# Attention and graph mixing on one core: another place for a run's last blocks, and x centred row by row on ScalarE

## The chip, the cores and the metric

One core of a Trainium2 chip runs the whole computation. The metric is the device time of one execution in microseconds. Engines work side by side, each on its own queue of instructions: TensorE (PE, with its weight loads PEld) multiplies matrices, VectorE (DVE) and ScalarE (ACT) do elementwise work and row sums, GpSimd (POOL) does the powers and starts most transfers, SyncE (SP) starts transfers and here also passes marks between TensorE instructions. Engines wait for each other by semaphores.

## The reference

Two layers over x of 16 batches x 1024 nodes x 64 channels and a dense 1024 x 1024 matrix adj, all in float32:

```python
Q = einsum('bnc,oc->bno', x, Wq) + bq
K = einsum('bnc,oc->bno', x, Wk) + bk
V = einsum('bnc,oc->bno', x, Wv)
score = softmax(einsum('bnc,bmc->bnm', Q, K), axis=1)
out = einsum('bnm,bmc->bnc', einsum('bnm,mc->bnc', score, adj), V)
x = layernorm(x + out)
# layer 1, with support0 = support1 = adj
x1 = adj @ x;  x2 = 2 * adj @ x1 - x
out = concat([x, x1, x2, x1, x2]) @ weight + bias
x = layernorm(x + out)
```

layernorm takes the mean of a node's 64 channels away and divides by the standard deviation; it has no weights.

## The kernel before, in words

**Data.** Two batches are kept together as a pair p, 0 to 7, so a tile of x for one pair is 128 nodes x (8 node blocks x 2 batches x 64 channels). `rows(p)` sees it as 16 rows of 64 channels on each of the 128 partitions. Batch j of a pair lies on partitions 64j to 64j+63 of the transposed tiles.

**The attention loop** (L699 to L785) runs over steps (p, m): pair p, column block m of its scores, 63 steps. The product adj @ x stands in place of adj @ V; the value weights are applied behind it. Step (p, m) prepares the scores of the next step for both batches (`sc0` for j = 0, `sc1` for j = 1, each 128 x 1024 in PSUM), and uses the exponentials of its own. For each batch VectorE takes the maximum (L409) and ScalarE the exponential (L418), which also sums it. Of both sums VectorE makes the reciprocal `ri` (L425) and the scaled weights `us` (L427), with which TensorE accumulates the attention result (`weighted`, L439). The score tile of one batch is the same buffer in every step, so the scores of step m + 1 wait for the exponential of step m.

**TensorE in quarters.** All products of the loop are 64 x 64: an instruction reads partitions 0 to 63 or 64 to 127 (here called row half 0 and row half 1) and writes one column half. Scores of batch 0 and the weighted products with t = 0 use row half 0, those of batch 1 and t = 1 row half 1.

**Beside the attention** the same steps carry, each a piece at a time and written out in order by hand:

- a `Run` (L673): one block product of adj @ x or of the next hop, by a scheme with seven products in place of eight. `part(t, *ks)` issues the blocks ks of row half t. When the last blocks of t = 0 are out, `passed` (L662) puts an instruction on SyncE's queue that waits for them and raises a mark; the first blocks of t = 1, which add into the same bank, wait for that mark (`behind_mark`, L669). VectorE evicts the run in the next step (L293 to L299).
- a small product, `small_of` (L653): `values` at (p, 1), `project` at (p, 4), `mix` at (p, 0), (p, 2), (p, 3), (p, 5) from p = 2 on. It is made for batch 0 (`small0`) in the first half of the step and for batch 1 (`small1`) in the second half, both in the one bank that the run doesn't hold. The second waits until ScalarE and VectorE have taken the first out (`project`: L381 and L385), and the run of the next step takes the same bank.
- VectorE jobs in two dictionaries by step, `first_gap` and `second_gap` (L625): sums for the block scheme (L250), transposes (L346), and the layer norms: the mean of x before the attention result is added (`means`, L391), its removal (`centre`, L394), the variance (L480), the scaling (L496). In a step the jobs of `first_gap` stand on VectorE between the maxima of batch 0 and batch 1.

In six steps (`two_runs`) two runs are made and no small product.

**Order on ScalarE in a step:** evictions of a small product of batch 0, the exponential of batch 0, in (p, 7) a copy (L504), evictions of the small product of batch 1, the exponential of batch 1.

**Behind the loop** (from 408 us) the second layer's hops run as full-size products; that part is not touched. There L993 scales single rows of 64 channels on ScalarE.

Of the kernel before, what the change touches and what calls it, by code (L numbers as in the profile page):

```python
# [10 lines left out]
AF = mybir.ActivationFunctionType  # L11
# [15 lines left out]
def gnn_kernel(  # L27
# [13 lines left out]
    nc = tc.nc  # L41
    N, B, C = out.shape
    P = 128
    K8 = N // P
    NP = B // 2
    HP = NP // 2
    H = 512
    G = 16
# [27 lines left out]
    def f_other(name):  # L76

        return pf.tile([P, H], FP, tag=f"f{1 - f_last[0]}", name=name)

    def sc_tile(name):  # L80
        return psc.tile([P, N], FP, tag="sc", name=name)
# [153 lines left out]
    class Hop:  # L235
# [46 lines left out]
        def evict(self, po, n, group, copy=nc.vector.tensor_copy):  # L282
            for do in self.evictions(po, n, group, copy):
                do()
# [23 lines left out]
    XT, GT, ACC, PU, OT, SQ, RSTD, X0T, XM = ({} for _ in range(9))  # L308

    def by_block(t):  # L310

        return t.rearrange("c (k a n) -> c a k n", k=K8, a=A4)

    def by_place(t):
        return t.rearrange("c (a k n) -> c a k n", k=K8, a=A4)
# [8 lines left out]
    def rows(p):  # L324
        return xs[:, p].rearrange("p k (b c) -> p (k b) c", b=2)

    def xT(p):
        if p not in XT:
            XT[p] = att.tile([P, N], FP, tag="xT", name="xT")
        return XT[p]  # L330
# [11 lines left out]
    def transposed(p, dst, queue=nc.gpsimd):  # L342


        t = att.tile([P, N], FP, tag="t", name="blocks", bufs=1)
        nc.vector.transpose(  # L346
            t.rearrange("p (b k n) -> p k b n", b=A4, k=K8),
            xs[:, p].rearrange("p k (b n) -> p k b n", b=A4),
        )
        d = dram.tile([P, N], FP, tag="d", name="d")  # L350
        queue.dma_start(d, t)  # L351
        for b in range(A4):
            queue.dma_start(
                dst[32 * b : 32 * b + 32].rearrange("c (a w) -> c a w", a=A4),
                d.rearrange("(a c) (b w) -> b c a w", a=A4, b=A4)[b],
            )
# [36 lines left out]
    def centre(p):  # L393
# [2 lines left out]
            op0=ALU.mult, op1=ALU.add,  # L396
        )

    def scores(sc, p, m, j, h):

        for c in range(2):
            nc.tensor.matmul(  # L402
                sc[half[c], ts(h, H)], GT[p][half[j], c * H + m * C : c * H + (m + 1) * C],
                xT(p)[half[j], ts(h, H)], start=True, stop=True,
            )
# [15 lines left out]
    def scaled(p, m):  # L421

        es, sm = PU[p, m]
        ri = small.tile([P, 2], FP, tag="ri", name="ri")
        nc.vector.reciprocal(ri, sm)  # L425
        us = small.tile([P, 2, C], FP, tag="us", name="us")
        nc.vector.tensor_tensor(  # L427
            us, UY[:, m, ts(p, P)].rearrange("p (j c) -> p j c", j=2),
            ri[:, :, None].to_broadcast([P, 2, C]), ALU.mult,
        )  # L430
        PU[p, m] = (es, us)

    def weighted(p, m, t, h):

        if m == 0 and t == 0:
            ACC[p, h] = pacc.tile([P, H], FP, tag=f"acc{h}", name="acc")
        es, us = PU[p, m]
        made = [
            nc.tensor.matmul(  # L439
                ACC[p, h][half[j]], us[half[t], j], es[j][half[t], ts(h, H)],  # L440
                start=m == 0 and t == 0, stop=m == K8 - 1, skip_group_check=True,
            )
            for j in range(2)
        ]
        if h == 0 and (t or m):
            behind_mark(made, sum_mark.pop())
        if h == 1 and not (t and m == K8 - 1):
            sum_mark.append(passed(made))

    def attended(p, h):  # L450

        if h == 0:
            OT[p] = att.tile([P, N], FP, tag="oT", name="oT", bufs=1)
        nc.scalar.activation(half_block(OT[p], h), half_place(ACC.pop((p, h))), AF.Copy)
# [31 lines left out]
    def squared(p):  # L486
        SQ[p] = att.tile([P, G, C], FP, tag="t", name="sq", bufs=1)
        nc.scalar.activation(SQ[p], rows(p), AF.Square, scale=C**-0.5)
# [13 lines left out]
    def x0T_in_order(p):  # L502
        t = att.tile([P, N], FP, tag="o", name="x0T_k", bufs=1)
        nc.scalar.activation(by_block(t), by_place(X0T[p]), AF.Copy)  # L504
        X0T[p] = t
# [78 lines left out]
    bias = const.tile([P, C], FP, tag="bias", name="bias")  # L584
# [37 lines left out]
        runs += [(hop, n, g) for order, groups in orders for g in groups for n in order]  # L622
    two_runs = {(0, 1), (0, 2), (1, 0), (2, 7), (HP + 1, 6), (HP + 1, 7)}

    first_gap, second_gap = {}, {}  # L625

    def at(gap, step, do, *args):
        gap.setdefault(step, []).append(lambda: do(*args))
# [10 lines left out]
        at(first_gap, step, hop_z.sums, n)  # L639
    for p in range(NP):  # L640

        at(first_gap, {
            0: (0, 6), 1: (1, 0), 2: (2, 1), 3: (3, 1), 6: (HP + 1, 7), 7: (7, 1)
        }.get(p, (p, 0)), means, p)
        at(first_gap, {0: (1, 0)}.get(p, (p, 6)), centre, p)
        if p + 1 < NP:
            at(first_gap, (p + 1, 2), spread, p)
            at(first_gap, (p + 1, 3), normed, p)
            at(first_gap, (p + 1, 5 if p + 2 < NP else 4), x0T, p)
        if p + 2 < NP:  # L650
            at(first_gap, (p, 7), lambda p: transposed(p, xT(p)), p + 2)
# [47 lines left out]
    for p in range(NP):  # L699
        q = p - 1  # L700
        for m in range(K8):
            if (p, m) == (NP - 1, K8 - 1):
                break
            nxt = (p, m + 1) if m + 1 < K8 else (p + 1, 0)
            sc = sc_tile("sc0")
            scores(sc, *nxt, 0, 0)
            rest = []
            if tail:
                tail.part(1, 2, 3)
                rest = tail.evict()  # L710
            scores(sc, *nxt, 0, 1)
            if before:
                weighted(*before, 1, 0)
                if m == 0:
                    attended(q, 0)
            scaled(p, m)
            for evict in late:
                evict()
            late = []
            if m == 2 and p:  # L720
                squared(q)
            todo = [Run() for _ in range(2 if (p, m) in two_runs else 1)]
            if before:
                weighted(*before, 1, 1)
                PU.pop(before)
            todo[0].part(0, 0, 1)
            what = small_of.get((p, m))
            sc1 = sc_tile("sc1")
            if what:
                parts, by_scalar, by_vector = what[0](*what[1:], (0,), [f_other("small0")])  # L730
                parts[0]()
            scores(sc1, *nxt, 1, 0)
            if what:
                for do in parts[1:]:
                    do()
            else:
                todo[0].part(0, 2, 3)
            nm = maximum(sc)
            if m == 0 and before:
                attended(q, 1)  # L740
            if what:
                by_scalar()
            exps(*nxt, 0, sc, nm)
            if p and m == (7 if p < NP - 1 else 6):
                x0T_in_order(q)
            jobs = first_gap.get((p, m), []) + rest
            if what:
                jobs.insert(len(jobs) if what[0] is project else 0, by_vector)
            for do in jobs:
                do()  # L750
            scores(sc1, *nxt, 1, 1)
            if what:
                todo[0].part(0, 2, 3)
            elif len(todo) > 1:
                todo[1].part(0, 0, 1)
                todo[1].part(0, 2, 3)
                todo[0].part(1, 0, 1)
            nm = maximum(sc1)
            weighted(p, m, 0, 0)
            if what:  # L760
                parts, by_scalar, by_vector = what[0](*what[1:], (1,), [f_other("small1")])
                if what[0] is project:
                    todo[0].part(1, 0)
                parts[0]()
                by_scalar()
                exps(*nxt, 1, sc1, nm)
            elif len(todo) > 1:
                todo[0].part(1, 2, 3)
                exps(*nxt, 1, sc1, nm)
                for do in todo[0].evict():  # L770
                    do()
            else:
                exps(*nxt, 1, sc1, nm)
            weighted(p, m, 0, 1)
            if what:
                for do in parts[1:]:
                    do()
                by_vector()
            if what and what[0] is project:
                todo[0].part(1, 1)  # L780
            else:
                todo[-1].part(1, 0, 1)
            for do in second_gap.get((p, m), ()):
                do()
            tail, before = todo[-1], (p, m)  # L785
# [384 lines left out]
    for step_, (i, cols) in enumerate((  # L1170
# [3 lines left out]
        k, p, n = wide_step(4, 1, 0, i, cols)  # L1174
# [49 lines left out]
```

## Time and profile before

| what | value |
|---|---|
| time, median of 4 runs | 569.97 us (569.59 to 570.35) |
| profiled execution | 569.59 us, its span 567.8 us |
| TensorE clock granted, mean | 0.993 |
| TensorE busy | 98% |
| VectorE busy | 78% |
| ScalarE busy | 44% |
| GpSimd busy | 27% |
| L394, centring on VectorE | 8 x 1216 ns |
| L391, means on VectorE | 8 x 1206 ns |
| attention loop, first to last step | 35.6 to 408 us of the span |

Times in the timeline are microseconds from the start of the span: start, duration, engine, line, operation, result <- inputs, shapes, count; in brackets how long the engine stood idle before and for whom. A row of PE may hold two instructions, the two column halves, and rows of the two row halves overlap.

### The profile page before, as it was taken

What the parts mean: (1) busy time and instruction counts of PE and PEld (TensorE: products, weight loads), DVE (VectorE), ACT (ScalarE), POOL (GpSimd) and SP (SyncE); (2) the same over time, 40 slices, a digit from 0 to 9 for tenths busy, and PEclk for the clock granted to TensorE, in tenths of its full rate; (3) what the DMA queues carried; (4) which work ended last, traced back from release to release, by engine and by line L of the source; (5) the groups of instructions that cost most, each with busy time, mean ns of one, the idle gap of its engine ahead of it and who ended that gap; (6) DMA issues with size and microseconds to landing.
All of it is one profiled execution on the core that took longest, in us unless ns stands there. A gap on an engine that the chain in (4) does not pass through costs nothing.

```text
span 567.8 us, 14491 instructions
## 1 busy us (share of the span) xinstructions
PE 555.6 (98%) x6150; PEld 410.1 (72%) x6150; DVE 441.8 (78%) x722; ACT 249.7 (44%) x525; POOL 153.1 (27%) x145
## 2 busy tenths in 40 slices
PE   9999999999999999999999999999999999999992
PEld 7757677657677877767767786577678789888552
DVE  1789889788888988879788788898656565799784
ACT  1133454546656556555654655455532200141571
POOL 0001001211211202112121120102102994793784
PEclk9999999999999999999999999999999999999997
DMA  8902001022012003102201200200102400002943
GB/s 277 331 2 76 2 39 39 1 76 76 3 66 86 2 1 114 38 2 76 76 1 52 101 1 3 75 2 15 64 1 75 76 0 2 1 21 53 208 142 95
DMA packets 20994, 33.66 MB, mean 59 GB/s; under 512 B 3010, under 2 KB 12482, under 8 KB 20546
## 3 DMA queue, kind: packets, MB, share of 16 engines
q0 software_dynamic: 6880, 18.88, 11.5%
q1 hardware_dynamic: 14050, 13.86, 7.4%
q8 instruction: 48, 0.79, 0.6%
q14 instruction: 16, 0.13, 0.1%
HBM read 16.48 MB, written 12.06 MB: 50 GB/s over the span
## 4 chain that ended last, share of the span: by engine, by line
PE 89%; DVE 5%; ACT 2%; DMA 1%; issue 1%; SPq 0%; POOL 0%; POOLq 0%; ACTq 0%; DVEq 0%
PE p L268 20%; PE sc L402 18%; PE acc L439 17%; PE w L831 15%; PE small L517 3%; PE w L1139 3%; PE pu L258 3%; PE wide L831 3%; PE small L464 2%; PE small L367 2%; DVE nm L409 1%; PE pv L258 1%; PE p L258 1%; ACT e L418 1%; PE both L517 1%
## 5 line engine op out<-in xcount | busy, mean ns | idle before, releaser
L402 PE MATMUL sc<-xT,GT 64*64 64x512 f32 x1024 | 240.8, 591 | 0.4 <-ACT e L418 0.2
L439 PE MATMUL acc<-e,us 64*64 64x512 f32 x1008 | 239.6, 590 | 0.0
L418 ACT ACTIVATE e<-sc,nm 128x1024 f32<-128x1024 f32 x128 | 142.8, 1115 | 123.3 <-DVE nm L409 115.6
L409 DVE TENSOR_REDUCE nm<-sc 128x1 f32<-128x1024 f32 x128 | 155.6, 1216 | 2.6 <-PE sc L402 2.1
L439 PEld LDWEIGHTS acc<-e,us 64*64 64x64 f32 x1008 | 71.0, 133 | 23.9 <-issue 9.2
L483 POOL TENSOR_TENSOR rstd<-var,expo 128x16 f32<-128x16 f32 (+3 forms) x21 | 50.8, 2427 | 130.7 <-DVE var L481 130.6
L402 PEld LDWEIGHTS sc<-xT,GT 64*64 64x64 f32 x1024 | 69.7, 132 | 12.0 <-issue 5.2
L351 POOL DMA_DIRECT2D d<-blocks x14 | 8.4, 599 | 198.5 <-DVE blocks L346 198.5
L268 PE MATMUL p<-UY,aT 64*64 64x256 f32 x480 | 59.2, 377 | 0.0
L268 PE MATMUL p<-XB,S 64*64 64x256 f32 x480 | 57.8, 377 | 0.0
L268 PE MATMUL p<-UY,S 64*64 64x256 f32 x384 | 45.7, 378 | 0.0
L268 PE MATMUL p<-XB,aT 64*64 64x256 f32 x352 | 43.4, 377 | 0.0
L268 PEld LDWEIGHTS p<-UY,aT 64*64 64x64 f32 x480 | 33.6, 133 | 12.1 <-issue 1.8
L268 PEld LDWEIGHTS p<-XB,S 64*64 64x64 f32 x480 | 33.0, 133 | 12.2 <-issue 2.3
L517 PE MATMUL small<-w,x0T_k 64*64 64x192 f32 x384 | 39.7, 323 | 0.0
L517 PEld LDWEIGHTS small<-w,x0T_k 64*64 64x64 f32 x384 | 26.7, 133 | 12.5 <-issue 5.5
L268 PEld LDWEIGHTS p<-UY,S 64*64 64x64 f32 x384 | 27.2, 133 | 8.4 <-issue 1.2
L268 PE MATMUL p<-xs,aT 64*64 64x256 f32 x256 | 31.7, 378 | 0.0
L268 PEld LDWEIGHTS p<-XB,aT 64*64 64x64 f32 x352 | 25.5, 133 | 8.5 <-issue 1.9
L268 PE MATMUL p<-xs,S 64*64 64x256 f32 x256 | 31.1, 377 | 0.0
L844 ACT COPY own<-w 128x512 f32<-128x512 f32 x8 | 4.5, 588 | 54.6 <-PE w L831 54.6
L527 ACT ACTIVATE UY<-small 128x128 f32<-128x128 f32 x48 | 13.3, 278 | 31.0 <-PE small L517 31.0
(210 smaller groups left out, 944.7 us busy)
## 6 DMA issues: line engine op xcount, KB each, us to landing
d<-blocks POOLq DMA_DIRECT2D x14, 512.0 KB, 3.0
xs<-own POOLq DMA_DIRECT2D x8, 512.0 KB, 6.8
xT<-d POOLq DMA_DIRECT2D x28, 128.0 KB, 2.9
x0T<-d POOLq DMA_DIRECT2D x28, 128.0 KB, 2.9
out_dram<-xs SPq DMA_DIRECT2D x14, 256.0 KB, 2.2
xs<-in_x_dram SPq DMA_DIRECT2D x3, 1024.0 KB, 7.6
aT<-in_adjT_dram SPq DMA_DIRECT2D x8, 256.0 KB, 4.8
aT<-in_adjT_dram SPq DMA_DIRECT2D x4, 512.0 KB, 7.7
```

Source lines behind the costliest of these rows:

```text
L258: nc.tensor.matmul(po[t * w : (t + 1) * w], SIDE[n][:, k, j : j + w], self.side[n][:, :, k, :], start=start, stop=True, skip_group_check=True,
L268: nc.tensor.matmul(po[half[c]], SIDE[n][half[t], k, i * P + c * C : i * P + (c + 1) * C], self.side[n][half[t], :, k, :], start=t == 0 and ...
L367: nc.tensor.matmul(t[half[b]], g2[half[j], half[j]], xT(p)[half[j], ts(b, H)], start=True, stop=True,)
L402: nc.tensor.matmul(sc[half[c], ts(h, H)], GT[p][half[j], c * H + m * C : c * H + (m + 1) * C], xT(p)[half[j], ts(h, H)], start=True, stop= ...
L409: nc.vector.tensor_reduce(nm, sc, AX.X, ALU.max, negate=True)
L418: nc.scalar.activation(e, sc, AF.Exp, bias=nm, accum_out=sm[:, j : j + 1])
L439: nc.tensor.matmul(ACC[p, h][half[j]], us[half[t], j], es[j][half[t], ts(h, H)], start=m == 0 and t == 0, stop=m == K8 - 1, skip_group_che ...
L483: nc.gpsimd.tensor_tensor(rstd, var, expo[:, 0:n], ALU.pow)
L517: nc.tensor.matmul(t[half[c], 0:3, k], X0T[p][half[j], n : n + C], w3[half[j]], start=True, stop=True,)
L527: nc.scalar.activation(part(UY, j), t[:, 0], AF.Copy)
L831: nc.tensor.matmul(po[:, ts(g, b.shape[1] * P)], a[:, k, ts(g, P)], b[:, :, k, :], start=start and g == 0 and k == 0, stop=True, skip_grou ...
L1139: nc.tensor.matmul(po, SIDE[n][:, k, ts(i, P)], B_F[n][:, k, cols], start=k == 0, stop=k == K4 - 1)
```

## The change

Three things change.

1. In a step with a small product, the run's last blocks of the first half, `part(0, 2, 3)` on row half 0, are issued ahead of `scores(sc1, ..., 1, 1)` on row half 1 instead of behind them. Steps without a small product had this order already.
2. x of pairs 1 to 7 is centred by ScalarE in place of VectorE. ScalarE multiplies the 16 row sums by -1/64 and then handles each row of 64 channels in an instruction of its own, with the mean as a bias per partition: 8 rows in (p, 1) and 8 in (p, 6), for pair 7 in (7, 1) and (7, 4). In a step they are issued behind the exponential of batch 0 and ahead of the evictions and the exponential of batch 1. Pair 0 stays on VectorE.
3. The row sums (`means`) are taken in other steps: for pairs 2 to 6 at (p - 1, 6), for pair 7 at (5, 0); pairs 0 and 1 stay at (0, 6) and (1, 0).

```diff
+    def centre_rows(p, b):
+
+        if b == 0:
+            nc.scalar.mul(XM[p], XM[p], -1.0 / C)
+        for i in range(G // 2 * b, G // 2 * (b + 1)):
+            nc.scalar.activation(rows(p)[:, i], rows(p)[:, i], AF.Identity, bias=XM[p][:, i : i + 1])
...
-        at(first_gap, {
-            0: (0, 6), 1: (1, 0), 2: (2, 1), 3: (3, 1), 6: (HP + 1, 7), 7: (7, 1)
-        }.get(p, (p, 0)), means, p)
-        at(first_gap, {0: (1, 0)}.get(p, (p, 6)), centre, p)
+        at(first_gap, {0: (0, 6), 1: (1, 0), 7: (HP + 1, 0)}.get(p, (p - 1, 6)), means, p)
+        if p == 0:
+            at(first_gap, (1, 0), centre, p)
+        else:
+            for b, m in enumerate((1, 6 if p + 1 < NP else 4)):
+                at(scalar_gap, (p, m), centre_rows, p, b)
...
             if p and m == (7 if p < NP - 1 else 6):
                 x0T_in_order(q)
+            for do in scalar_gap.get((p, m), ()):
+                do()
             jobs = first_gap.get((p, m), []) + rest
             if what:
                 jobs.insert(len(jobs) if what[0] is project else 0, by_vector)
             for do in jobs:
                 do()
-            scores(sc1, *nxt, 1, 1)
             if what:
                 todo[0].part(0, 2, 3)
-            elif len(todo) > 1:
+            scores(sc1, *nxt, 1, 1)
+            if len(todo) > 1:
                 todo[1].part(0, 0, 1)
                 todo[1].part(0, 2, 3)
                 todo[0].part(1, 0, 1)
```

`HP` is 4, `NP` 8, `G` 16, `C` 64; `scalar_gap` is a third dictionary by step.

More of the change, by code (lines that the diff above doesn't have):

```diff
@@ L623, in gnn_kernel @@
     two_runs = {(0, 1), (0, 2), (1, 0), (2, 7), (HP + 1, 6), (HP + 1, 7)}
-    first_gap, second_gap = {}, {}
+    first_gap, second_gap, scalar_gap = {}, {}, {}
     def at(gap, step, do, *args):
```

## The prediction

> **What bounds the kernel now.** I read the page's busy shares first, then the groups, the waits, and last the timeline of single steps of the attention loop, which fills 35.6 to 408 us of the span.
>
> ```profile
> PE 555.6 (98%) x6150; PEld 410.1 (72%) x6150; DVE 441.8 (78%) x722; ACT 249.7 (44%) x525; POOL 153.1 (27%) x145
> L418 ACT ACTIVATE e<-sc,nm 128x1024 f32<-128x1024 f32 x128 | 142.8, 1115 | 123.3 <-DVE nm L409 115.6
> L993 ACT ACTIVATE xs<-xs,rstd 128x64 f32<-128x64 f32 x64 | 15.8, 342 | 6.3 <-POOL rstd L483 6.3
> L394 DVE SCALAR_TENSOR_TENSOR xs<-xm,xs 128x1024 f32<-128x1024 f32 x8 | 9.7, 1216 | 0.0
> PEld p L268 <- SPq L664: 6.5, 17, 0.8
> ```
>
> PE is busy 98%, so only places where it stands still or runs on one row half can give time. A busy PE may be on one half only: products on row half 0 and row half 1 run beside each other. I added, step by step, the starts' spacings (512 columns 0.43 us, 256 columns 0.215, 192 columns 0.16, two column halves at once) and compared with each step's length. Steps with mix products lose about 0.03 us; steps with values 0.2; with project 0.28, and the step behind project 0.31. Steps (6,6) to (7,1) lose 2.1 together: there VectorE runs without a pause.
>
> This is PE's timeline in project step (4,4), the second part of it:
>
> ```profile
> 249.43 0.41 PE L268 MATMUL p<-XB,S 64*64 64x256 f32 x2
> 249.58 0.59 PE L402 MATMUL sc<-xT,GT 64*64 64x512 f32 x2
> 250.01 0.59 PE L402 MATMUL sc<-xT,GT 64*64 64x512 f32 x2
> 250.08 0.41 PE L268 MATMUL p<-XB,S 64*64 64x256 f32 x2
> 250.44 0.59 PE L402 MATMUL sc<-xT,GT 64*64 64x512 f32 x2
> 251.23 0.43 PE L268 MATMUL p<-XB,S 64*64 64x256 f32 x2
> 251.71 0.59 PE L367 MATMUL small<-xT,g 64*64 64x512 f32 x2
> ```
>
> and, of its weight loads:
>
> ```profile
> 251.23 0.20 PEld L268 LDWEIGHTS p<-XB,S 64*64 64x64 f32 x4 [0.76 <-SPq L664]
> ```
>
> The blocks p of 249.43 to 250.08 are the run's last blocks of the first half (row half 0). In the code they stand behind all scores of row half 1 (starts 249.58 to 250.44), yet start before the last of them. The blocks at 251.23 (row half 1) wait for SyncE's mark (`passed`, L662) of the first ones. Those were over by 250.08 + 0.38 = 250.46, but the mark comes only after the scores are over, 250.44 + 0.59 = 251.03. So starts pass each other between row halves, while completion is reported in the order of the code. Row half 1 is free at 250.44 + 0.43 = 250.87 and stands until 251.23.
>
> And this is the loop that links the steps, in (4,6) and (4,7), the centring of x[4] on VectorE (L394) included:
>
> ```profile
> 262.09 1.22 DVE L394 SCALAR_TENSOR_TENSOR xs<-xm,xs 128x1024 f32<-128x1024 f32 x1
> 262.29 1.11 ACT L418 ACTIVATE e<-sc,nm 128x1024 f32<-128x1024 f32 x1 [1.87 <-DVE nm L409]
> 263.32 1.23 DVE L409 TENSOR_REDUCE nm<-sc 128x1 f32<-128x1024 f32 x1
> 264.64 1.11 ACT L418 ACTIVATE e<-sc,nm 128x1024 f32<-128x1024 f32 x1 [1.14 <-DVE nm L409]
> 265.88 0.17 DVE L425 RECIPROCAL ri<-es 128x2 f32<-128x2 f32 x1
> 266.29 1.22 DVE L409 TENSOR_REDUCE nm<-sc 128x1 f32<-128x1024 f32 x1
> 267.63 1.11 ACT L418 ACTIVATE e<-sc,nm 128x1024 f32<-128x1024 f32 x1 [1.78 <-DVE nm L409]
> 268.88 0.14 PEld L402 LDWEIGHTS sc<-xT,GT 64*64 64x64 f32 x2
> ```
>
> The second exponential (264.64, sums read until 265.84) releases the reciprocal at 265.88; behind it on VectorE stands the next maximum (266.29), which releases the next first exponential (267.63 to 268.74), which frees the score bank that PE writes at 268.88. PE could have begun at 268.78 (the product of 268.35 plus 0.43). This chain has no slack.
>
> **Part 1, the order on PE.** It touches the 38 steps with small products (7 values, 7 project, 24 mix). No product is added or removed, and on each row half the order stays. In mix steps the halves are already full. In a project step the mark now follows scores that end at 249.58 + 0.59 = 250.17 and blocks that end at 250.46, so it is there before 250.87: row half 1 gains 251.23 - 250.87 = 0.36. The small product behind it (251.71) moves to 251.35, unless its bank is late: the VectorE copy of the first half's result ends at 250.38 + 0.76 = 251.14, in time. ScalarE's copy (252.78) and VectorE's second copy (253.50), and so the bank for which row half 0 waits in the next step (254.31), follow by 0.36. Both halves gain 0.36. In p = 2, 3, 5 and 6 the first copies end at 156.56, 204.73, 297.61 and 347.50, each over 0.4 before the small product at 157.15, 205.25, 298.18 and 348.06: same gain. In p = 0 and 1 these copies end at 64.98 and 110.62, right before the small products at 65.03 and 110.73: nothing. Sum 5 x 0.36 = 1.8 us gained. From below: nothing, if another wait takes the mark's place; from above 7 x 0.36 = 2.5.
>
> A rule speaks here. The Trainium skill's page "TensorE: Matmul & The Clock Gate", section "The mechanism" of Part 3, says that matmuls start and end strictly in program order and only weight loads are pulled ahead. By it the old order would hold row half 0 from about 249.43 until 250.44, the new one would not, and 0.4 us in each of 38 steps, 15 us, would be an estimate of the gain. The starts above contradict the first half of it; the late mark agrees with the second.
>
> **Part 2, x centred by ScalarE.** VectorE loses seven L394, 7 x 1.216 = 8.5 us. ScalarE gets 112 rows of 128x64 and seven products of 128x16. The nearest row is L993, the same shape in place with one operand per partition: 16 take 3.95 us, so (3.95 - 0.34) / 15 = 0.24 apart. From below, L527 and L528 (128x128 with constants) start 0.16 apart; from above, 0.34, if nothing overlaps. I take 0.24, the same form and shape.
>
> The rows stand on ScalarE between the two exponentials of a step. The next instruction starts 1.10 behind the first exponential (267.63 to L504 at 268.73), eight rows take 8 x 0.24 = 1.92: the second starts at least 3.02 behind the first. Before, at (p,6): p = 1: 121.37 to 123.62, 2.25; p = 2: 2.45; p = 3: 215.83 to 218.18, 2.35; p = 4: 2.35; p = 5: 3.38; p = 6: 2.91; p = 7 at (7,4): 394.53 to 396.88, 2.35. Late by 0.77, 0.57, 0.67, 0.67, 0, 0.11, 0.67.
>
> The chain above passes this on to PE: p = 1 at (2,0) 0.77 (old start 127.86, PE free 127.84); p = 3 and 4 0.67 each; p = 6 0.11. For p = 2 the step (2,7) has two runs: the exponential of 173.06 to 174.17 frees the bank 1.7 before PE needs it at 175.94, so nothing. For p = 7 a wait for PE hides most: the first exponential of 399.84 starts at 400.51, ends at 401.62 and frees the bank 0.13 later (268.74 to 268.88 above), PE wants it at 401.65: 0.1. Sum 0.77 + 2 x 0.67 + 0.11 + 0.1 = 2.3 us lost.
>
> At (p,1) the second exponential comes 2.43 behind the first (231.97 to 234.40) and would come 3.13 behind (0.11 more for the small product); the 0.7 is covered, because the reciprocal of (4,2) waits for PE's blocks until 236.37 anyway and the late sums are there at 236.30. If that cover were gone, 7 x 0.7 = 4.9 would show.
>
> **Part 3, the means.** Same seven reductions of 1.21, now mostly at (p-1,6), where L394 stood, so (1,6) to (5,6) carry the same VectorE work. Relieved are (2,1), (3,1), (4,0), (5,7), (6,6), (7,1), (7,6), 1.2 each. Only (6,6) and (7,1) lie in the late stretch; there the rows hold the second exponential to 362.24 instead of 362.13, so the freed VectorE time meets a busy ScalarE: no gain. No DMA moves; SP's and POOL's queues keep their order.
>
> **Sum.** Profiled execution 569.59 (span 567.8 and 1.8 around it) - 1.8 + 2.3 = 570.1; the median of the runs is 0.4 above it: 570.5 us.
>
> **The rivals.**
> Faster: rows at 0.16. Then the second exponential comes 1.10 + 1.28 = 2.38 behind the first, late by 0.13, 0.03 and 0.03 only, and in (6,6) it comes 0.53 sooner because VectorE is free. 1.8 - 0.2 + 0.5 = 2.1 gained: 567.9. For it: constants-only forms show 0.16. Against: the same shape shows 0.24.
> Slower: the mark is no longer late, but the row-half-1 blocks then wait for something else, such as their weights behind the scores; part 1 gives nothing and part 2 stays: 572.3. It decides once less than 0.3 of the 0.36 comes in each step. For it: the gain rests on one reading of the mark; against: five steps show the same gap.
> Slower by far: in the new order the scores are held behind the blocks, 226.35 instead of 226.11 in mix step (4,0), 0.24 in 31 steps, 7.4 us: 577. Against: the old order shows starts passing three pairs.
> The change does nothing: the two orders act alike, and the rows find room: 570.0; it lies within my forecast's own range.
>
> **How the numbers follow.** Forecast 0.46, faster rival 0.20, slower rival 0.30, slower by far 0.04. About 0.2%, 1.1 us, is what a measurement of this kernel tells from no change. Forecast: 0.40 within, 0.04 above, 0.02 below; each of the first two rivals leaves 0.02 within. Faster 0.20, same 0.44, slower 0.36. The forecast's own range is 569.2 to 571.6; with the rivals at 567.9 and 572.3 and 0.5 around them, 567.4 to 572.9. Rows at 0.34 would cost some 6 us and lie outside.
>
> **What would show it.** Right: no wait of PE's weights for SyncE's mark in project steps, second exponentials 3.0 behind the first at (p,6), PE standing at (2,0), (4,0), (5,0) some 0.7 us longer, rows 0.24 apart, VectorE's busy time down by 8.5 and ScalarE's up by 27. Wrong: rows much nearer to each other or further apart, project steps as long as before, or mix steps longer than 5.81.

## The result and the profile after

The changed kernel takes 570.38 us (median of 33 runs, 569.89 to 571.18), the kernel before 569.95 us (53 runs, 569.29 to 570.57): ratio 1.0008, 95% interval 1.0004 to 1.0013. That is 0.4 us slower, where 0.5 was forecast. The profiled execution took 570.32 us with a span of 568.5 us.

So little is left because a gain and a loss of over 2 us each nearly cancel. The page of the changed kernel, busy shares and two groups (busy time, mean of one, idle time before and what ended it):

```profile
PE 555.2 (98%) x6150; PEld 406.2 (71%) x6150; DVE 434.5 (76%) x715; ACT 276.4 (49%) x644; POOL 153.1 (27%) x145
L425 ACT ACTIVATE e<-sc,nm 128x1024 f32<-128x1024 f32 x128 | 142.6, 1114 | 102.5 <-DVE nm L416 95.2
L404 ACT ACTIVATE xs<-xs,xm 128x64 f32<-128x64 f32 x112 | 28.3, 339 | 0.2
```

VectorE has 7.3 us less to do and ScalarE 26.7 us more. (8.5 less was forecast for VectorE, from whole durations; these overlap in part with the instruction behind: 359.02 + 1.22 against the next start at 360.15 in (6,6) before.) 112 rows are busy for 28.3 us, 0.25 each. ScalarE waits 20 us less in front of the exponentials (95.2 for VectorE's maxima, 115.6 before), because rows now fill the wait.

The waits of TensorE's weight loads, first of the changed kernel, then the same line of the kernel before that the prediction didn't show (total, times, longest):

```profile
PEld sc L409 <- ACT e L425: 8.9, 18, 0.7
PEld p L268 <- SPq L674: 2.6, 11, 0.3
```

```profile
PEld sc L402 <- ACT e L418: 3.4, 7, 0.6
```

Waits for SyncE's mark went from 6.5 us to 2.6, waits of the scores for an exponential from 3.4 to 8.9. These are the two sides of the change, except that the new order alone already brings the second number to 4.4 (order_project, below).

**The gain, on TensorE's timeline.** Project step (4,4) of the changed kernel, the same piece as before (start, duration; the rows of the weighted products, L446, are left out):

```profile
250.39 0.41 PE L268 MATMUL p<-XB,S 64*64 64x256 f32 x2
250.54 0.60 PE L409 MATMUL sc<-xT,GT 64*64 64x512 f32 x2
250.60 0.63 PE L268 MATMUL p<-XB,S 64*64 64x256 f32 x4
250.97 0.60 PE L409 MATMUL sc<-xT,GT 64*64 64x512 f32 x2
251.03 0.41 PE L268 MATMUL p<-XB,S 64*64 64x256 f32 x2
251.40 0.59 PE L409 MATMUL sc<-xT,GT 64*64 64x512 f32 x2
251.82 0.60 PE L268 MATMUL p<-XB,S 64*64 64x256 f32 x4
252.25 0.60 PE L367 MATMUL small<-xT,g 64*64 64x512 f32 x2
```

Blocks and scores start in the same interleaving as before: the order in the code changed, the order of starts on the chip did not. But the blocks of row half 1 now start at 251.82, when that half comes free (251.40 + 0.43), and no mark holds them.

**The loss, on the loop between the steps.** (4,6) and (4,7) of the changed kernel, the rows of this chain alone:

```profile
262.64 1.21 DVE L391 TENSOR_REDUCE xm<-xs 128x16 f32<-128x1024 f32 x1
262.84 1.11 ACT L425 ACTIVATE e<-sc,nm 128x1024 f32<-128x1024 f32 x1 [1.87 <-DVE nm L416]
263.87 1.23 DVE L416 TENSOR_REDUCE nm<-sc 128x1 f32<-128x1024 f32 x1
263.94 2.02 ACT L404 ACTIVATE xs<-xs,xm 128x64 f32<-128x64 f32 x8
265.86 1.10 ACT L425 ACTIVATE e<-sc,nm 128x1024 f32<-128x1024 f32 x1
267.09 0.17 DVE L432 RECIPROCAL ri<-es 128x2 f32<-128x2 f32 x1 [0.74 <-ACT e L425]
267.50 1.22 DVE L416 TENSOR_REDUCE nm<-sc 128x1 f32<-128x1024 f32 x1
268.83 1.11 ACT L425 ACTIVATE e<-sc,nm 128x1024 f32<-128x1024 f32 x1 [1.78 <-DVE nm L416]
270.09 0.14 PEld L409 LDWEIGHTS sc<-xT,GT 64*64 64x64 f32 x2 [0.64 <-ACT e L425]
```

The maximum was over at 263.87 + 1.23 = 265.10, but the second exponential starts only at 265.86, behind the eight rows: 3.02 behind the first one (2.35 before). From there each step of the chain is as far behind the one ahead of it as before, and TensorE's weight load for the next scores waits 0.64 us for the exponential.

Step by step, the distance from the first scores of a step to those of the next, read from TensorE's timeline of each run (us; the last five columns are the experiments below, taken from one profile each):

| step | before | changed | order_project | rows_alone | rows_split | rows_late | rows_12 |
|---|---|---|---|---|---|---|---|
| (4,4) | 6.27 | 6.12 | 6.12 | 6.27 | 6.12 | 6.12 | 6.12 |
| (4,5) | 6.19 | 5.93 | 5.93 | 6.19 | 5.93 | 5.93 | 5.93 |
| (1,7) | 5.23 | 6.00 | 5.22 | 5.98 | 5.21 | 5.23 | 6.93 |
| (2,7) | 6.89 | 7.22 | 6.89 | 7.21 | 6.89 | 6.89 | 8.16 |
| (3,7) | 5.27 | 5.93 | 5.26 | 5.91 | 5.26 | 5.28 | 6.87 |
| (4,7) | 5.27 | 5.93 | 5.26 | 5.92 | 5.27 | 5.29 | 6.86 |
| (6,7) | 5.90 | 5.99 | 5.90 | 5.98 | 5.21 | 5.21 | 6.94 |
| (7,1) | 6.55 | 6.56 | 6.55 | 6.55 | 6.42 | 6.15 | 6.55 |
| (7,5) | 5.86 | 5.97 | 5.86 | 5.96 | 5.86 | 5.86 | 6.91 |

A project step and the one behind it are 0.15 + 0.26 = 0.41 shorter, and 0.40 to 0.42 in each of the pairs 2 to 6, some 2.05 us in all. The steps that end with the late exponential are longer by 0.77, 0.33, 0.66, 0.66, 0.09 and 0.11, 2.6 us in all. Of the steps that the table leaves out, (1,3) and (3,1) are 0.06 and 0.09 shorter; (7,2) and (7,3) are 0.06 and 0.05 longer and (7,4) is 0.11 shorter.

### The profile page after: what moved, and what is told of

Same layout as the page of the kernel before. It is cut to its first block, busy times and chain, and to the rows that moved or that the text cites. A ratio compares the mean times of both kernels' runs of the same rounds, so it can differ in the third digit from the quotient of the medians.

```text
span 568.5 us, 14578 instructions
## 1 busy us (share of the span) xinstructions
PE 555.2 (98%) x6150; PEld 406.2 (71%) x6150; DVE 434.5 (76%) x715; ACT 276.4 (49%) x644; POOL 153.1 (27%) x145
## 4 chain that ended last, share of the span: by engine, by line
PE 82%; DVE 7%; ACT 5%; DMA 2%; issue 1%; SPq 1%; POOL 0%; POOLq 0%; ACTq 0%; DVEq 0%
PE p L268 18%; PE sc L409 17%; PE w L843 14%; PE acc L446 14%; PE small L524 3%; PE w L1151 3%; DVE nm L416 3%; PE wide L843 2%; ACT e L425 2%; PE small L471 2%; ACT xs L404 1%; PE pv L258 1%; PE pu L258 1%; PE small L367 1%; DMA early<-in_wqT_dram 1%
## 5 line engine op out<-in xcount | busy, mean ns | idle before, releaser
L446 PE MATMUL acc<-e,us 64*64 64x512 f32 x1008 | 238.7, 590 | 0.0
L425 ACT ACTIVATE e<-sc,nm 128x1024 f32<-128x1024 f32 x128 | 142.6, 1114 | 102.5 <-DVE nm L416 95.2
L446 PEld LDWEIGHTS acc<-e,us 64*64 64x64 f32 x1008 | 70.2, 133 | 23.2 <-issue 8.6
L409 PEld LDWEIGHTS sc<-xT,GT 64*64 64x64 f32 x1024 | 68.5, 132 | 16.8 <-ACT e L425 8.9
L404 ACT ACTIVATE xs<-xs,xm 128x64 f32<-128x64 f32 x112 | 28.3, 339 | 0.2
```

The source lines that it names most:

```text
L404: nc.scalar.activation(rows(p)[:, i], rows(p)[:, i], AF.Identity, bias=XM[p][:, i : i + 1])
L409: nc.tensor.matmul(sc[half[c], ts(h, H)], GT[p][half[j], c * H + m * C : c * H + (m + 1) * C], xT(p)[half[j], ts(h, H)], start=True, stop= ...
L425: nc.scalar.activation(e, sc, AF.Exp, bias=nm, accum_out=sm[:, j : j + 1])
L446: nc.tensor.matmul(ACC[p, h][half[j]], us[half[t], j], es[j][half[t], ts(h, H)], start=m == 0 and t == 0, stop=m == K8 - 1, skip_group_che ...
```

## The experiments

All of these kernels were timed in five rounds against the kernel before on the same chip.

### Part 1 alone, and where its gain lies

The new order in all 38 steps (order_all), in the seven project steps only (order_project), and in the other 31 only (order_rest). Of the kernel before:

```diff
-            scores(sc1, *nxt, 1, 1)
             if what:                   # order_project: if what and what[0] is project
                 todo[0].part(0, 2, 3)
-            elif len(todo) > 1:
+            scores(sc1, *nxt, 1, 1)
+            if len(todo) > 1:
```

In order_project and order_rest the remaining steps with a small product issue the blocks behind the scores, as before.

> The kernel before with part 1 of the change alone: the run's last blocks of row half 0 ahead of the scores of row half 1 in all 38 steps with a small product. Theory (the mark is late because completion is reported in the order of the code): the project steps of pairs 2 to 6 and the steps behind them get 0.41 us shorter each (what the changed kernel's trace shows of both parts together), 2.0 us in all, about 567.9. Rival 1 (the project steps got shorter because ScalarE or VectorE were relieved, not because of the order): no gain, 570.0. Rival 2 (products start strictly in the order of the code): 0.4 us in each of the 38 steps, 15 us, 555.

> The new order in the 7 project steps alone; values and mix steps keep the old order. Theory: the whole gain of the order is here, 2.0 us, 567.9, the same as with all 38 steps. Rival (the gain is spread over all steps with small products): 7 of 38 parts of it, under 0.4 us.

> The new order in the 7 values and 24 mix steps alone; project steps keep the old order. Theory: nothing, 570.0 within 0.3 us, because in these steps the mark is needed only behind the weighted products of the second half, some 2 us later. Rival (scores held behind the blocks in the new order): up to 0.24 us in each of 31 steps, 7 us slower. Rival (products start strictly in the order of the code): 12 us faster.

| kernel | median | before | ratio, 95% interval |
|---|---|---|---|
| order_all | 567.84 | 569.80 | 0.9964 (0.9952 to 0.9977) |
| order_project | 567.61 | 569.80 | 0.9962 (0.9948 to 0.9975) |
| order_rest | 569.91 | 569.80 | 1.0001 (0.9992 to 1.0010) |

The gain is 2.0 to 2.2 us, and all of it comes from seven of the 38 steps. The waits of weight loads for SyncE's mark say the same, first in order_project, then in order_rest:

```profile
PEld p L268 <- SPq L664: 2.1, 10, 0.3
```

```profile
PEld p L268 <- SPq L664: 6.5, 17, 0.8
```

VectorE and ScalarE do in order_project what they did before (441.6 and 249.4 us), so their relief has no part in it. The rule that products start strictly in the order of the code would have given 12 us in order_rest; nothing came. That the mark was late because completion is reported in the order of the code fits the times of before (blocks over at 250.46, scores at 251.03, mark taken and weights loaded at 251.23) and the gap that is gone. The trace's record of the one semaphore that both the blocks and the scores raise says it directly: before, it rises at 251.06 and at 251.15, but not when the blocks are over, and SyncE passes the mark at 251.17. In the changed kernel it rises at 251.46, with the end of the blocks (251.45), and again at 252.01, behind the scores. So the report of the blocks stood behind that of the scores ahead of them in the code. (The ends of products are modelled; by which part of the chip the report is held, the runs don't show.)

### Parts 2 and 3 alone

The changed kernel with the old order on TensorE.

> Parts 2 and 3 of the change alone, the old order on TensorE: x of pairs 1 to 7 centred by ScalarE and the means in the new steps. Theory (eight rows of 0.24 us hold the second exponential of a step, and by it the next step's sums, maximum, first exponential and scores): 2.4 to 2.7 us slower, 572.5; steps (1,7) to (2,0), (2,7), (3,7) and (4,7) longer by 0.8, 0.3, 0.7 and 0.7. Rival (the rows find room, the relieved VectorE gives time): 570 or less.

572.33 us against 569.80, ratio 1.0044 (1.0031 to 1.0057): 2.5 us slower. The table has the same steps longer by the same amounts as in the changed kernel: 0.75, 0.32, 0.64, 0.65, 0.08 and 0.10. -2.1 and +2.5 add up to +0.4, which is what the whole change measures, and in each step of the table the two effects add up to the changed kernel's within 0.03 us: as far as this shows, the parts do not act on each other.

### Place or load

The same rows on the same engine, at another place in its queue. rows_split puts four of the eight rows of (p,6) and (7,4) behind the second exponential, rows_late all eight; the eight rows of (p,1) stay where they are. `centre_rows(p, lo, hi)` now takes the rows lo to hi, and `scalar_late` is a dictionary like `scalar_gap` for jobs behind the second exponential:

```diff
-            for b, m in enumerate((1, 6 if p + 1 < NP else 4)):
-                at(scalar_gap, (p, m), centre_rows, p, b)
+            m = 6 if p + 1 < NP else 4
+            at(scalar_gap, (p, 1), centre_rows, p, 0, 8)
+            at(scalar_gap, (p, m), centre_rows, p, 8, 12)     # not in rows_late
+            at(scalar_late, (p, m), centre_rows, p, 12, 16)   # rows_late: 8, 16
...
             else:
                 exps(*nxt, 1, sc1, nm)
+            for do in scalar_late.get((p, m), ()):
+                do()
             weighted(p, m, 0, 1)
```

> The changed kernel, with the eight rows of (p,6) and (7,4) cut in two: four between the two exponentials as before, four behind the second. ScalarE's load, VectorE's and the order on TensorE are those of the changed kernel. Theory (the place in the queue costs, not the load): the second exponential comes 1.10 + 4 x 0.24 = 2.06 behind the first and so waits for its maximum again; the loss of 2.4 to 2.7 us is gone, and in (6,6) the second exponential comes up to 0.85 earlier than before the change because VectorE no longer centres: 2.0 to 2.9 us faster than before, 567.0 to 567.9. Rival (112 rows are too much for ScalarE wherever they stand): about 570.

> The changed kernel with all eight rows of (p,6) and (7,4) behind the second exponential. Theory: between the end of the second exponential and the next first one lie 1.9 us (124.72 to 126.60, 265.74 to 267.63 before), eight rows take 1.92, so the next first exponential is late by 0.1 to 0.2 in four places: 567.3 to 568.3. Rival (the load costs): about 570.

rows_split: 567.05 us against 569.87, ratio 0.9952 (0.9938 to 0.9965). rows_late: 566.78, ratio 0.9947 (0.9934 to 0.9959). The two can't be told apart, both are 0.5% faster than the kernel before, and ScalarE is as busy as in the changed kernel (275.7 us in rows_late). The load costs nothing where it stands in a wait. ScalarE in steps (4,6) and (4,7) of rows_late:

```profile
261.01 1.11 ACT L425 ACTIVATE e<-sc,nm 128x1024 f32<-128x1024 f32 x1 [1.88 <-DVE nm L416]
...
263.36 1.11 ACT L425 ACTIVATE e<-sc,nm 128x1024 f32<-128x1024 f32 x1 [1.15 <-DVE nm L416]
...
264.46 2.01 ACT L404 ACTIVATE xs<-xs,xm 128x64 f32<-128x64 f32 x8
266.38 1.10 ACT L425 ACTIVATE e<-sc,nm 128x1024 f32<-128x1024 f32 x1
```

The second exponential is 2.35 behind the first again, and the rows fill what was a wait of 1.78 us behind it. My expectation for rows_late, 567.3 to 568.3, missed: the kernel is faster. I had put the next first exponential 0.1 to 0.2 late in four places; the steps (3,7) and (4,7) are only 0.02 to 0.03 longer than in order_project, and (7,1) gains 0.27 more than in rows_split.

### More rows at the same place

Twelve rows between the two exponentials of (p,6) and (7,4), four in (p,1):

```diff
+            at(scalar_gap, (p, 1), centre_rows, p, 0, 4)
+            at(scalar_gap, (p, m), centre_rows, p, 4, 16)
```

> The changed kernel with four rows in (p,1) and twelve between the two exponentials of (p,6) and (7,4). Theory: four more rows hold the second exponential 0.96 us longer in each of these seven steps; in p = 1, 2, 3, 4, 6 and 7 all or most of it comes through to TensorE, in p = 5 some 0.6: 4 to 6.5 us slower than the changed kernel, 574.4 to 577. Rival (the loss in the changed kernel has another cause than these rows): no more than 1 us slower than the changed kernel.

575.88 us against 569.87, ratio 1.0107 (1.0093 to 1.0121): 5.6 us above the changed kernel by the two ratios (0.0099 of 569.9). ScalarE in (4,6):

```profile
265.63 1.11 ACT L425 ACTIVATE e<-sc,nm 128x1024 f32<-128x1024 f32 x1 [1.86 <-DVE nm L416]
266.74 2.96 ACT L404 ACTIVATE xs<-xs,xm 128x64 f32<-128x64 f32 x12
269.60 1.10 ACT L425 ACTIVATE e<-sc,nm 128x1024 f32<-128x1024 f32 x1
```

The exponentials are 3.97 apart, 0.95 more than with eight rows, and the steps (1,7), (2,7), (3,7), (4,7), (6,7) and (7,5) are 0.93 to 0.95 longer than in the changed kernel: six times 0.94 is the 5.6. What a row between the exponentials costs there is its 0.24 us, undiminished. Pair 5, for which I had expected some 0.6, shows nothing: its exponentials in (5,6) are 0.6 further apart than in the changed kernel (3.97 against 3.37), but (5,7) takes 6.89 in every run.

### What VectorE's relief is worth

No centring of pairs 1 to 7 at all, so the output lacks it:

```diff
-            for b, m in enumerate((1, 6 if p + 1 < NP else 4)):
-                at(scalar_gap, (p, m), centre_rows, p, b)
+            pass
```

> The changed kernel without any centring of pairs 1 to 7: neither VectorE nor ScalarE takes the mean away, so the output lacks it; the order on TensorE and the places of the row sums are those of the changed kernel. It shows what VectorE's relief of seven times 1.2 us is worth when nothing takes its place. Theory: little, because only the stretch from (6,6) to (7,1) waits for VectorE: the order's 2.0 us and 0.9 to 1.5 more, 566.5 to 567.1. Rival (VectorE's relief is worth its whole time in the loop): 8.5 us more, 559.5.

566.54 us against 569.87, ratio 0.9943 (0.9931 to 0.9956). That is 3.2 us, of which the order has 2.0 to 2.2; the relief of VectorE by seven times 1.2 us is worth some 1.1 us. rows_late, which does the centring, is level with it. The place is (6,6), as ScalarE's second exponential shows, first in rows_none and then in rows_late, each with the first one ahead of it:

```profile
357.11 1.11 ACT L425 ACTIVATE e<-sc,nm 128x1024 f32<-128x1024 f32 x1 [1.77 <-DVE nm L416]
358.90 1.11 ACT L425 ACTIVATE e<-sc,nm 128x1024 f32<-128x1024 f32 x1 [0.58 <-DVE nm L416]
```

```profile
357.11 1.11 ACT L425 ACTIVATE e<-sc,nm 128x1024 f32<-128x1024 f32 x1 [1.77 <-DVE nm L416]
358.90 1.11 ACT L425 ACTIVATE e<-sc,nm 128x1024 f32<-128x1024 f32 x1 [0.58 <-DVE nm L416]
360.00 2.01 ACT L404 ACTIVATE xs<-xs,xm 128x64 f32<-128x64 f32 x8
```

They are 1.79 apart in both (before 2.91, in the changed kernel 3.02). In the changed kernel the rows stood in this very gap and took back what VectorE had given; step (6,7) is 5.21 long here and 5.99 there. (7,1) gains 0.40 as well. The row sums of pair 7 have left that step, but they are not the reason: they left it in the changed kernel too, whose (7,1) is as long as before, and the 0.40 is already there at the step's first maximum (3.08 behind its first scores in rows_none, 3.48 before), ahead of the place where the sums stood. It is carried on from (6,6).

## Why the prediction was right

The sign, the size and both mechanisms held. That the sum came within 0.1 us of the result is in part luck: the gain was put 0.25 us too small and the loss 0.2, and these cancel. Term by term:

- **Order, project steps.** Forecast 5 x 0.36 = 1.8, measured 5 x 0.41 = 2.0 in the profile and 2.0 to 2.2 in the runs alone. Pairs 0 and 1 gained nothing, as forecast from their late bank ((1,4): 6.16 before, 6.15 after). The 0.05 that was left out is the restart: behind a wait, the first two products of a row half start 0.27 apart (251.23 and 251.50 before), not 0.22. Row half 0, whose products stood behind the waiting weight load, restarted as well (251.35 and 251.83, 0.48 apart for 512 columns and not 0.43).
- **Order, other steps.** Forecast nothing, order_rest shows nothing within 0.1%.
- **Rows.** Forecast 0.24 apart; the eight take 2.02 us, (2.02 - 0.34) / 7 = 0.24. Second exponentials 3.02 behind the first, as forecast. Steps (1,7), (3,7), (4,7), (6,7) and, for p = 7, (7,5) longer by 0.77, 0.66, 0.66, 0.09 and 0.11 against 0.77, 0.67, 0.67, 0.11 and 0.1.
- **Rows in (p,1).** The second exponentials come 3.27 behind the first from p = 2 on, not 3.13: the small product ahead of the rows takes 0.24 of ScalarE's time (378.88 to 379.12 in (7,1)) and not 0.11. The cover held all the same: the steps (p,1) and (p,2) of pairs 1 to 6 are none longer than before, and what (7,2) and (7,3) lose, (7,4) gives back.
- **The term that was mis-sized.** For p = 2 the prediction said "so nothing", because the first exponential frees its bank 1.7 us early. The step (2,7) is 0.33 longer all the same. It looked at one of the two score banks only. The late second exponential also frees the bank of the second scores late, and their weight load stands ahead of the blocks of the other row half in TensorE's queue. The changed kernel in (2,7), the second exponential of the step before and the rows around it:

```profile
171.09 1.10 ACT L425 ACTIVATE e<-sc,nm 128x1024 f32<-128x1024 f32 x1
171.63 0.60 PE L268 MATMUL p<-XB,S 64*64 64x256 f32 x4
172.33 0.14 PEld L409 LDWEIGHTS sc<-xT,GT 64*64 64x64 f32 x2 [0.56 <-ACT e L425]
172.35 0.43 PE L268 MATMUL p<-XB,S 64*64 64x256 f32 x2
172.42 0.60 PE L409 MATMUL sc<-xT,GT 64*64 64x512 f32 x2
172.62 0.60 PE L268 MATMUL p<-XB,S 64*64 64x256 f32 x4
```

  and the same place before, 0.43 earlier in the span, where the blocks follow each other without a pause:

```profile
171.21 0.60 PE L268 MATMUL p<-XB,S 64*64 64x256 f32 x4
171.64 0.60 PE L268 MATMUL p<-XB,S 64*64 64x256 f32 x4
171.99 0.60 PE L402 MATMUL sc<-xT,GT 64*64 64x512 f32 x2
```

  The scores themselves lose nothing: their row half is busy until 172.42. The blocks on row half 0 could have started at 171.63 + 2 x 0.22 = 172.07 and stand until the weight load ahead of them has its semaphore at 172.33. That is 0.28, and 0.05 for the restart. In (1,7), (3,7) and (4,7) the same wait is inside the longer one that follows. The wait is gone where the second exponential is on time: (2,7) takes 6.89 in rows_split and rows_late. With this term the forecast loss is 2.6 and not 2.3; the steps measure 2.6, and less the 0.15 that (1,3) and (3,1) gave back this is the 2.5 of rows_alone.
- **Means.** Nothing that their new places cost or gave shows: (2,1), (4,0) and (5,7) are as long as before. (3,1) is 0.09 shorter, but only in the kernels whose second exponential in (2,6) is late (not in rows_split, rows_late and rows_none, where the sums have left (3,1) too), so it is not their relief. A kernel with the means moved and all else as before was not run.
- **The rivals.** Faster (rows at 0.16): the rows took 0.24. Slower (the mark's place taken by another wait): excluded by order_project. Slower by far (scores held behind the blocks): excluded by order_rest. The weighing of the Trainium skill's page "TensorE: Matmul & The Clock Gate", section "The mechanism", came out for the trace: across row halves, starts pass each other in both orders of the code.

What moved least is not settled. (1,3) is 0.06 shorter in every run with rows in (1,1), (3,1) 0.09 as said, and (7,2) to (7,4) shift against each other in every run with eight rows in (7,1); no run was made for the reasons.

## What to carry to other kernels

Work that is moved to an engine with idle time is free where that engine waits for something that it can't hasten, or where what it delays has slack (the rows in (p,1)); the same eight rows of each pair cost 2.5 us in front of an exponential that a chain needs and nothing behind it. Two parts of a change that each look sensible can cancel, so time each alone: here one part was worth 0.4% and hid a placing that cost as much, and the same change with eight rows of each pair moved behind one instruction is 0.5% faster than the kernel before. For a wait, look at what stands behind the waiting instruction in its queue, on the other row half too, and at every buffer that the late instruction frees.

## What the runs showed of the hardware beyond what was expected

- A weight load that waits for a semaphore on one row half holds the products of the other half that stand behind it in the code: row half 0 stood 0.28 us in (2,7), though it needed nothing from the exponential, and 0.20 us in (4,4) before, behind the load that waited for the mark (251.15 to 251.35). Products that only wait for a busy row half did not hold the others (250.08 before 250.44 in the prediction's timeline).
- A row half that restarts behind a wait starts its second product 0.05 us later than in a running series (251.23 to 251.50, against 0.22 in the series).
- ScalarE's rows of 128x64 start 0.24 us apart with a bias per partition (L404), as they did with a scale per partition (L993), though one alone takes 0.34.
